# Gathers of 127 rows instead of 128 in a graph layer's aggregation

## The chip, the core and the metric

The kernel runs on one core of a Trainium2 chip. The metric is the device time of one execution in microseconds, the median of several runs.

## What is computed

One graph layer over 50,000 nodes of 128 features and 1,650,000 edges that are sorted by destination. Every edge carries its source's row through one of two linear maps, chosen by the edge's type; the messages are summed by destination, the node's own row is mapped and added, and relu, a residual and a layer norm follow.

```
Xs = X[src]
m_data = Xs @ W_data.T + b_data
m_ctrl = Xs @ W_control.T + b_control
msg = jnp.where((edge_types == 0)[:, None], m_data, m_ctrl)
agg = jax.ops.segment_sum(msg, dst, num_segments=X.shape[0])
out = agg + (X @ W_self.T + b_self)
x = _layernorm(x + relu(out), axis=-1)
```

All of it is float32; in the graph, 800,000 random pairs are taken both ways and each node has a loop.

## The kernel before

The maps are linear, so the kernel sums source rows first and maps the sums. Edges are cut into chunks of 128 (12,891 of them, the last with 80 edges), 14 chunks to a step, 921 steps, 20 steps to a group. Since edges are sorted, a step's destinations fall into a window of W = 64 nodes that starts at `base`.

For each chunk, `products` (L158 to L171) issues one indirect DMA on GpSimd's queue (L166): edge e's source row of x, 512 bytes, lands in partition e of a tile y. TensorE multiplies y by a one-hot matrix of 128 columns, 64 nodes by two edge types (L169), and accumulates over the step's 14 chunks in PSUM. A last product with ones (L170) turns the counts of edges into a multiple of the bias. A float32 product shows as two MATMUL instructions.

The one-hot comes from `onehot` (L146 to L155), on VectorE: one comparison for all 14 chunks (L151) and one reduction for the counts (L154), three steps ahead of its use (AHEAD). `columns` (L123 to L138) makes, once per group, the column number of each edge, and the smallest and largest of them for a check at the end. `carry` (L185 to L189) adds to a step's sums what the step before had beyond its own window; `layer` (L199 to L206) maps the sums, `moments` and `store` do the norm and write 64 rows.

The order is written out by hand at the end of `straight` (L228 to L250): in the loop over steps come the carry and transpose of the step before, the load of x's rows for four steps later (`window`, SP's queue), in the middle of a group the three loads of edges for the next one (`load_edges`, L82 to L86, SP's queue), then this step's products, the layer of the step before, the moments of the one before that, the one-hot of three steps ahead, and the store. GpSimd has hardly anything but the gathers. The tile pool of y has 5 * S = 70 buffers, and edge tiles have two.

If the check at the end finds a destination outside of its window, `general` (from L277 on) computes all again in another way; on this graph it isn't run.

The edge arrays are laid out on the host as [128, chunks]: partition p of column c is edge 128 c + p.

## Time and profile before

| | before |
|---|---|
| median of 2 runs | 18587.68 us (18585.29 to 18590.06) |
| profiled execution, its own time | 16137.76 us |
| its span, first to last instruction | 16136.0 us |
| PE busy | 12545.0 us (78%) |
| POOL busy | 12182.1 us (75%), 12,891 gathers of 945 ns |
| VectorE busy | 6216.3 us (39%) |
| granted clock of TensorE | 0.52 |
| moved by DMA | 935.47 MB, 58 GB/s |

The profile shows one execution. PE is TensorE's products and PEld its weight loads, DVE is VectorE, ACT ScalarE, POOL GpSimd, SP the engine that issues plain DMAs. Of an indirect DMA on POOL, the busy time is what the engine spends on the instruction, and the transfer comes after it. A group's line gives the line number, engine, operation, tiles (out<-in) and count, then busy time, mean ns of one, and the idle time of the engine just before with what ended it. The runs take longer than the profiled execution, so both are given.

### The profile page before, as it was taken

How to read it: one execution, taken by the hardware profiler on the slowest of the kernel's cores; microseconds unless marked ns; L12 is line 12 of the kernel's file. 1: busy time of each engine (PE TensorE's matmuls, PEld its weight loads, DVE VectorE, ACT ScalarE, POOL GpSimd, SP SyncE). 2: the span in 40 equal slices, each digit the busy share in tenths (PEclk: the TensorE clock that was granted, in tenths of full speed). 3: DMA queues.
4: the chain of work that ended last, by engine and by line, in shares of the span. 5: the costliest groups of instructions: out<-in, count | busy, mean ns of one | idle time of the engine just before them, and what ended most of it. 6: DMA issues, size and time to landing. Idle time of an engine off the chain costs nothing.

```text
span 16136.0 us, 131172 instructions
## 1 busy us (share of the span) xinstructions
PE 12545.0 (78%) x39604; PEld 8196.0 (51%) x39605; DVE 6216.3 (39%) x7631; ACT 470.5 (3%) x1848; POOL 12182.1 (75%) x12899
## 2 busy tenths in 40 slices
PE   7777777777777777777777777777777777777777
PEld 4555555555555555555555555555555555555554
DVE  4333333333333333333333333333333333333333
ACT  0000000000000000000000000000000000000000
POOL 7777777777777777777777777777777777777777
PEclk5555555555555555555555555555555555555555
DMA  2222222222222222222222222222222222222222
GB/s 60 58 58 59 58 58 58 58 58 59 58 58 58 58 58 58 59 58 58 58 58 58 59 58 58 58 58 58 58 59 58 58 58 58 58 58 59 58 58 55
DMA packets 581475, 935.47 MB, mean 58 GB/s; under 512 B 238051, under 2 KB 374374, under 8 KB 580758
## 3 DMA queue, kind: packets, MB, share of 16 engines
q0 software_dynamic: 412512, 845.63, 20.1%
q1 hardware_dynamic: 167808, 81.17, 1.9%
q8 instruction: 318, 5.21, 0.1%
q14 instruction: 399, 3.27, 0.1%
q10 hardware_dynamic: 438, 0.20, 0.0%
HBM read 895.86 MB, written 30.18 MB: 57 GB/s over the span
## 4 chain that ended last, share of the span: by engine, by line
DMA 43%; PE 39%; issue 14%; POOL 4%; POOLq 0%; DVE 0%; ACT 0%; ACTq 0%
DMA y<-in_x,idx_g 43%; PE acc L169 17%; PE po L205 6%; PE po L206 6%; POOL y L166 4%; PE po L202 3%; PE po L203 3%; PE acc L170 2%; PE px L194 1%; POOLq L166 0%; DMA idx_g<-in_src_t 0%; DVE o L225 0%; ACT sd L217 0%; DVE h L211 0%; POOL num L107 0%
## 5 line engine op out<-in xcount | busy, mean ns | idle before, releaser
L166 POOL DMA_INDIRECT y<-in_x,idx_g x12891 | 12181.1, 945 | 3928.8 <-issue 1768.6
L169 PE MATMUL acc<-oh,y 128*128 128x128 f32 x25782 | 8534.1, 469 | 3568.3 <-DMA y<-in_x,idx_g 3543.7
L169 PEld LDWEIGHTS acc<-oh,y 128*128 128x128 f32 x25782 | 6054.6, 312 | 5885.3 <-DMA y<-in_x,idx_g 5709.2
L189 DVE TENSOR_TENSOR sums<-acc,sums 128x256 f32<-128x256 f32 x921 | 391.0, 425 | 6746.0 <-PE acc L170 6746.0
L154 DVE TENSOR_REDUCE cnt<-oh 128x128 f32<-128x1792 f32 x921 | 2922.5, 3173 | 31.7
L151 DVE TENSOR_TENSOR oh<-col_g,num_ps 128x1792 f32<-128x1792 f32 x921 | 1824.3, 1981 | 0.0
L211 DVE SCALAR_TENSOR_TENSOR h<-po,xw 64x128 f32<-64x128 f32 x921 | 260.7, 283 | 3013.4 <-PE po L206 3013.4
L205 PE MATMUL po<-wmsgT,sums 128*64 128x128 f32 x3684 | 1269.8, 448 | 3.3 <-DVE sums L189 3.3
L206 PE MATMUL po<-bias,sums 1*64 1x128 f32 x3684 | 1260.6, 444 | 0.0
L205 PEld LDWEIGHTS po<-wmsgT,sums 128*64 128x64 f32 x3684 | 531.7, 204 | 610.9 <-issue 606.9
L206 PEld LDWEIGHTS po<-bias,sums 1*64 1x64 f32 x3684 | 523.7, 202 | 608.8 <-issue 608.8
L196 ACT COPY xT<-px 128x64 f32<-128x64 f32 x921 | 195.9, 213 | 15325.7 <-PE px L194 15325.7
L202 PE MATMUL po<-wselfT,xT 128*64 128x128 f32 x1842 | 635.6, 449 | 0.2 <-ACT xT L196 0.2
L203 PE MATMUL po<-bias,ones 1*64 1x128 f32 x1842 | 630.3, 444 | 0.0
L170 PE MATMUL acc<-cnt,ones 128*128 128x128 f32 x1842 | 584.1, 421 | 0.0
L170 PEld LDWEIGHTS acc<-cnt,ones 128*128 128x128 f32 x1842 | 503.5, 333 | 0.0
L203 PEld LDWEIGHTS po<-bias,ones 1*64 1x64 f32 x1842 | 261.9, 202 | 304.4 <-issue 304.4
L202 PEld LDWEIGHTS po<-wselfT,xT 128*64 128x64 f32 x1842 | 266.6, 205 | 206.9 <-issue 206.5
L194 PE MATMUL px<-ident,xw 64*128 64x64 f32 x921 | 336.1, 365 | 0.0
L225 DVE TENSOR_SCALAR o<-h,mv,rstd 64x128 f32<-64x128 f32 x921 | 317.6, 345 | 33.3
L194 PEld LDWEIGHTS px<-ident,xw 64*128 64x128 f32 x921 | 163.9, 178 | 303.6 <-issue 303.4
L217 ACT ACTIVATE sd<-mv,eps 64x1 f32<-64x1 f32 x921 | 271.3, 295 | 322.1 <-DVE mv L215 318.2
(56 smaller groups left out, 667.8 us busy)
## 6 DMA issues: line engine op xcount, KB each, us to landing
y<-in_x,idx_g POOLq DMA_INDIRECT x12891, 2.5
xw<-in_x SPq DMA_DIRECT2D x921, 32.0 KB
out<-o SPq DMA_DIRECT2D x921, 32.0 KB
idx_g<-in_src_t SPq DMA_DIRECT2D x47, 140.0 KB
d_g<-in_dst_t SPq DMA_DIRECT2D x47, 140.0 KB
t_g<-in_edge_type_t SPq DMA_DIRECT2D x47, 140.0 KB
first_i<-in_dst_first SPq DMA_DIRECT2D x1, 460.5 KB
w_sb<-in_L_gnn_W_data ACTq DMA_DIRECT2D x1, 64.0 KB
```

The source lines that it names most:

```text
L151: nc.vector.tensor_tensor(oh[:, :n, :], col_g[g][:, i, :n, None].to_broadcast([P, n, 2 * W]), num_ps[:, None, :].to_broadcast([P, n, 2 * W ...
L154: nc.vector.tensor_reduce(cnt, oh[:, :n, :].rearrange("p s w -> p w s"), AX.X, ALU.add)
L166: nc.gpsimd.indirect_dma_start(out=y[:r], out_offset=None, in_=x, in_offset=bass.IndirectOffsetOnAxis(ap=idx_g[g][:r, i, k:k + 1], axis=0))
L169: nc.tensor.matmul(flat[:, :2 * W], y[:r], oh[:r, k, :], start=k == 0, stop=k == n - 1)
L170: nc.tensor.matmul(flat[:, 2 * W:], ones, cnt, start=True, stop=True)
L189: nc.vector.tensor_tensor(sums[s % RING][:, :, :W], accs.pop(s), sums[(s - 1) % RING][:, :, bass.ds(d, W)], op=ALU.add)
L194: nc.tensor.transpose(px, xws[s], c["ident"][:W, :W])
L202: nc.tensor.matmul(po, xTs.pop(s), c["wselfT"], start=True, stop=False)
L203: nc.tensor.matmul(po, ones[0:1, :W], bias[:, 2, :], start=False, stop=False)
L205: nc.tensor.matmul(po, a[:, t, :W], c["wmsgT"][:, t * D:(t + 1) * D], start=False, stop=False)
L206: nc.tensor.matmul(po, a[0:1, 2 + t, :W], bias[:, t, :], start=False, stop=t == 1)
L225: nc.vector.tensor_scalar(o, hs.pop(s), mv[:, 0:1], rstd, op0=ALU.subtract, op1=ALU.mult)
```

## The change

A new constant R = 127 takes the place of 128 as the number of edges in a chunk. There are 12,993 chunks, the last with 16 edges, and 929 steps. All tiles of edges and the one-hot have 127 partitions, as has y; products contract over 127 rows. The tile of the check's numbers, which is reduced over all 128 partitions at the end, is set to zero first. The host lays the edges out as [127, chunks]. The other path (`general`) keeps its chunks of 128.

```diff
+R = 127
+NCHUNK = -(-E // R)
+LAST = E - (NCHUNK - 1) * R
...
     stats = keep.tile([P, 2, GROUPS], F32, name="stats")
+    nc.vector.memset(stats, 0.0)
...
-            t = eds.tile([P, GS, S], I32, name=name)
+            t = eds.tile([R, GS, S], I32, name=name)
             nc.sync.dma_start(t.rearrange("p a b -> p (a b)"), a[:, g * GS * S:(g + 1) * GS * S])
...
-        oh = ohp.tile([P, S, 2 * W], F32, name="oh")
-        nc.vector.tensor_tensor(oh[:, :n, :], col_g[g][:, i, :n, None].to_broadcast([P, n, 2 * W]),
-                                num_ps[:, None, :].to_broadcast([P, n, 2 * W]), op=ALU.is_equal)
-        cnt = ohp.tile([P, 2 * W], F32, name="cnt")
+        oh = ohp.tile([R, S, 2 * W], F32, name="oh")
+        nc.vector.tensor_tensor(oh[:, :n, :], col_g[g][:, i, :n, None].to_broadcast([R, n, 2 * W]),
+                                num_ps[:R, None, :].to_broadcast([R, n, 2 * W]), op=ALU.is_equal)
+        cnt = ohp.tile([R, 2 * W], F32, name="cnt")
...
-            r = LAST if s * S + k == NCHUNK - 1 else P
-            y = gat.tile([P, D], F32, name="y")
+            r = LAST if s * S + k == NCHUNK - 1 else R
+            y = gat.tile([R, D], F32, name="y")
             nc.gpsimd.indirect_dma_start(
                 out=y[:r], out_offset=None, in_=x,
                 in_offset=bass.IndirectOffsetOnAxis(ap=idx_g[g][:r, i, k:k + 1], axis=0))
             nc.tensor.matmul(flat[:, :2 * W], y[:r], oh[:r, k, :], start=k == 0, stop=k == n - 1)
-        nc.tensor.matmul(flat[:, 2 * W:], ones, cnt, start=True, stop=True)
+        nc.tensor.matmul(flat[:, 2 * W:], ones[:R], cnt, start=True, stop=True)
...
-        arrays[k + "_t"] = np.ascontiguousarray(a[:TCH * CH].reshape(TCH, CH).T)
-    arrays["dst_first"] = np.ascontiguousarray(arrays["dst"][:STEPS * S * CH:S * CH])
+        arrays[k + "_t"] = np.ascontiguousarray(a[:TCH * R].reshape(TCH, R).T)
+    arrays["dst_first"] = np.ascontiguousarray(arrays["dst"][:STEPS * S * R:S * R])
```

The tiles of `columns` change in the same way.

More of the change, by code (lines that the diff above doesn't have):

```diff
@@ L27 @@
 CH = 128
-NCHUNK = -(-E // CH)
-LAST = E - (NCHUNK - 1) * CH
 DST_PAD = 65536
+R = 127
+NCHUNK = -(-E // R)
+LAST = E - (NCHUNK - 1) * R
 W = 64
@@ L41 @@
 U = 35
-CPP = -(-(NCHUNK + U) // P)
+CPP = -(-(-(-E // CH) + U) // P)
 NCH = CPP * P
@@ L125, in columns @@
         d, t = d_g.pop(g), t_g.pop(g)
-        rel = eds.tile([P, GS, S], F32, name="rel")
-        nc.vector.tensor_tensor(rel, d, base[:, g * GS:(g + 1) * GS, None].to_broadcast([P, GS, S]),
+        rel = eds.tile([R, GS, S], F32, name="rel")
+        nc.vector.tensor_tensor(rel, d, base[:R, g * GS:(g + 1) * GS, None].to_broadcast([R, GS, S]),
                                 op=ALU.subtract)
-        col = eds.tile([P, GS, S], F32, name="col_g")
+        col = eds.tile([R, GS, S], F32, name="col_g")
         nc.vector.tensor_scalar(col, t, 0.0, float(W), op0=ALU.not_equal, op1=ALU.mult)
@@ L133, in columns @@
         if g == GROUPS - 1:
-            chk = eds.tile([P, GS, S], F32, name="chk")
+            chk = eds.tile([R, GS, S], F32, name="chk")
             nc.vector.scalar_tensor_tensor(chk, d, float(DST_PAD), rel, op0=ALU.is_lt, op1=ALU.mult)
-        nc.vector.tensor_reduce(stats[:, 0, g:g + 1], chk.rearrange("p a b -> p (a b)"), AX.X, ALU.min)
-        nc.vector.tensor_reduce(stats[:, 1, g:g + 1], chk.rearrange("p a b -> p (a b)"), AX.X, ALU.max)
+        nc.vector.tensor_reduce(stats[:R, 0, g:g + 1], chk.rearrange("p a b -> p (a b)"), AX.X, ALU.min)
+        nc.vector.tensor_reduce(stats[:R, 1, g:g + 1], chk.rearrange("p a b -> p (a b)"), AX.X, ALU.max)
         col_g[g] = col
@@ L559 @@
     for k, pad in (("src", 0), ("dst", DST_PAD), ("edge_type_2", 0)):
-        a = np.pad(np.asarray(inputs[k], dtype=np.int32), (0, max(EPAD, TCH * CH) - E), constant_values=pad)
+        a = np.pad(np.asarray(inputs[k], dtype=np.int32), (0, max(EPAD, TCH * R) - E), constant_values=pad)
         arrays[k] = np.ascontiguousarray(a[:EPAD])
-        arrays[k + "_t"] = np.ascontiguousarray(a[:TCH * CH].reshape(TCH, CH).T)
-    arrays["dst_first"] = np.ascontiguousarray(arrays["dst"][:STEPS * S * CH:S * CH])
+        arrays[k + "_t"] = np.ascontiguousarray(a[:TCH * R].reshape(TCH, R).T)
+    arrays["dst_first"] = np.ascontiguousarray(arrays["dst"][:STEPS * S * R:S * R])
     nc = bacc.Bacc("TRN2", target_bir_lowering=False, num_devices=1)
```

## The prediction

> **What bounds the kernel now.** I read the page's busy shares and costliest groups first, then what POOL waits for, the transfers, and two stretches of the timeline. Page, parts 1 and 3 to 5:

> ```profile
> PE 12545.0 (78%) x39604; PEld 8196.0 (51%) x39605; DVE 6216.3 (39%) x7631; ACT 470.5 (3%) x1848; POOL 12182.1 (75%) x12899
> ...
> q0 software_dynamic: 412512, 845.63, 20.1%
> q1 hardware_dynamic: 167808, 81.17, 1.9%
> ...
> DMA 43%; PE 39%; issue 14%; POOL 4%; POOLq 0%; DVE 0%; ACT 0%; ACTq 0%
> ...
> L166 POOL DMA_INDIRECT y<-in_x,idx_g x12891 | 12181.1, 945 | 3928.8 <-issue 1768.6
> L169 PE MATMUL acc<-oh,y 128*128 128x128 f32 x25782 | 8534.1, 469 | 3568.3 <-DMA y<-in_x,idx_g 3543.7
> ```

> PE has the larger busy share, and the chain names transfers (43%) and PE (39%). The groups say otherwise: PE's gap before L169 is a wait for y, and POOL's busy time plus its gap before L166, 12181.1 + 3928.8 = 16109.9 us, is the span (16136.0) but for 26 us. The waits of POOL:

> ```profile
> POOL y L166 <- issue: 1768.6, 5806, 0.3
> POOL y L166 <- PE acc L169: 1226.1, 4025, 0.3
> POOL y L166 <- DMA y<-in_x,idx_g: 694.2, 2279, 0.3
> ```

> Whatever releaser is named, no wait is over 0.3 us: 3928.8 / 12891 = 0.305 us stands before every gather, so it is a fixed part of issuing one. The period is 16110 / 12891 = 1.250 us, from first to last. The end of the timeline (start, length, engine, line), where the last gather has 80 rows and not 128:

> ```profile
> 16108.20 0.94 POOL L166 DMA_INDIRECT y<-in_x,idx_g  x1 [0.30 <-issue]
> ...
> 16109.45 0.94 POOL L166 DMA_INDIRECT y<-in_x,idx_g  x1 [0.30 <-issue]
> ...
> 16110.70 0.91 POOL L166 DMA_INDIRECT y<-in_x,idx_g  x1 [0.30 <-issue]
> ...
> 16113.19 0.80 PE L169 MATMUL acc<-oh,y 80*128 80x128 f32 x2 [0.41 <-DMA y<-in_x,idx_g]
> ```

> The view of tile y gives 907 ns as the shortest gather and 945 as the median. So 48 rows fewer save 38 ns: 0.8 ns a row, or 12.7 ns for each 16 rows. Rows taken linearly cost 8 x 12.7 = 101 ns, and 844 ns don't depend on them. That is the number on which the forecast turns: the change takes one row in 128 and perhaps fifteen engines in sixteen.

> How far PE is behind, in the timeline:

> ```profile
> 8000.70 0.64 PE L170 MATMUL acc<-cnt,ones 128*128 128x128 f32 x2
> ...
> 8005.26 3.31 PE L169 MATMUL acc<-oh,y 128*128 128x128 f32 x12
> ...
> 8022.88 3.05 PE L169 MATMUL acc<-oh,y 128*128 128x128 f32 x12
> ```

> What PE does once per step takes from 8000.70 to 8005.26, 4.56 us. Twelve unstarved products take 3.05 us, (3.05 - 0.42) / 11 = 0.239 each; 28 are 6.7 us. PE needs 11.3 us of the step's 14 x 1.25 = 17.5: a floor of 0.80 us per gather. DVE needs 6216.3 / 921 = 6.7 us per step.

> [...] 412512 / 12891 = 32 packets a gather and 845.63 MB / 12891 = 65.6 KB, that is sixteen 4 KB packets and sixteen of 4 bytes. For 127 rows nothing here shows it. [...]

> **The change, part by part.**

> *More gathers.* 1,650,000 / 127 gives 12993 for 12891: 102 more, 0.79%. At 1.250 us each that is +127 us of the profiled span. The last one has 16 rows. Steps are 929 for 921; the eight add 8 x 11.3 us to PE and 8 x 6.7 to DVE, behind POOL's period, so nothing. If POOL fell below 0.80 us they'd count 90 us on PE.

> *One row less per gather.* 1 x 0.8 ns x 12993 = -10 us if cost goes by rows. If it goes by rounds of 16, 127 rows are still eight and nothing is saved.

> *One engine for sixteen.* Not in the trace. Bounds: below, the 844 + 305 ns contain per-engine work of which 15/16 goes, 1.08 us; but PE then stops it at 0.80 us per gather. Above, the 12.7 ns are a round that serves sixteen engines at once, and one engine takes 127 rounds: (127 - 8) x 12.7 = +1511 ns. I take zero, from between the bounds: [...]

> *The transfer itself.* It has 20.1% of 16 x 16136 / 12891 = 4.03 us of engine time a gather. On one engine this is serial: landing goes from 2.5 to about 2.5 + 4.03 x 15/16 = 6.3 us. 70 buffers of y hold 70 x 1.25 = 87 us, [...]. Hidden; [...].

> *Edge loads (L85).* 127 partitions on SP's queue: [...]. q1's packets take 1.9% of 16 x 16136 / 167808 = 29 ns at 484 bytes on average; 127 of 1120 bytes are an estimated 4 to 9 us, three loads 11 to 26. They are issued ten steps (175 us) early, three SP issues as before, and SP's queue behind them holds rows of x four steps ahead. Hidden, but for the first: gather one waits for idx_g, now 2.3 us, so +4 to +9 once.

> *DVE and PE on 127 partitions.* Same free sizes, so the same time; the memset of stats is one instruction. No new wait stands in any loop.

> Sum, profiled: +127 + 6 - 10 to 0, so about 16136 + 128 = 16264. The median of the runs is 18587.68, 1.152 times the profiled execution's 16137.76, or 1.442 us a gather. [...] I carry the ratio: 18587.68 x 12993 / 12891 = 18735 us, +0.8%.

> **The cases.**

> *U, nothing but more gathers* (24%): 18735, own range 18600 to 18950. [...]

> *F2, a pass over sixteen engines falls away* (23%). If the 0.305 us before each gather is such a pass, 15/16 of it is 0.286: 0.964 us, 12993 x 0.964 = 12.53 ms, 14430 us in runs; with part of it, up to 18300. For it: the gap is constant and the same for all releasers. [...] It beats 2% from 0.035 us saved.

> *F1, [...]* (13%): POOL drops to PE's floor, 929 x 11.3 us = 10.5 ms, 12100 us in runs. For it: 844 of 945 ns don't follow rows. [...]

> *S1, rounds per engine* (20%), the other side: at L166 each gather makes 127 rounds of 12.7 ns, so 1.250 + 1.511 = 2.761 us; 12993 of them 35.9 ms, 41300 us in runs. It decides from 0.13 ns per extra round (0.015 us for 2%). [...] Against it: one measured point, the 80-row gather.

> *S2, the same with cheaper rounds* (17%): half of S1's, 2.0 us, 26.0 ms, 30000 us; from 19000 to 36000.

> *S3, [...]* (3%): 4.03 us, 52.4 ms, 60300 us.

> **How the numbers follow.** Faster 0.36 (F1, F2), within 2% 0.24 (U), slower 0.40 (S1 to S3). About 2% is what a measurement of this kernel can tell from no change. U is the likeliest single case, hence 18735, though both signs weigh more than it; its own range is above. Range 13000 to 42000: below lies most of F1 (0.10), above S3 and S1's upper part (0.08).

> **What would show it.** L166's mean near 945 and 0.30 before it in a count of 12993: U. A shorter gap: F2; a shorter L166: F1, with PE's waits for y gone. An L166 of 1.5 to 2.5 us with PE waiting for y at every product: S. q0's packets tell k: 32 a gather with sixteen of about 4 KB either way, so landing decides: 2.5 us if spread, some 6 us on one engine. A profiled execution whose ratio to the runs isn't 1.15 would break my conversion. I am wrong wherever a 127-row gather takes POOL over 2% more or less than a 128-row one.

## The result, and the profile after

| | before | after |
|---|---|---|
| median of the runs | 18587.68 us | 37101.58 us (37101.0 to 37102.17, 2 runs) |
| profiled execution, its own time | 16137.76 us | 37101.0 us |
| span | 16136.0 us | 37099.2 us |
| gathers, POOL's time of one | 12,891 of 945 ns | 12,993 of 2548 ns |
| gather, issue to landing (median) | 2.5 us | 7.7 us |
| granted clock of TensorE | 0.52 | 0.50 |

The change makes the kernel slower: the ratio of the runs is 1.996 (95% interval 1.9874 to 2.0046). The runs of the kernel before differ between the comparisons, which were made on different chips: 16.14 ms in that of e1 to e4 below, 18.6 ms in the others. The kernel after took 37.1 ms in both of its comparisons, which were of the 18.6 ms kind. The profile of before is of a 16.14 ms execution, and whether that was on the chip of its two runs isn't known. So the two traces differ by a factor of 2.30.

The page of the kernel after, parts 1 and 3 to 5:

```profile
PE 14174.4 (38%) x39928; PEld 8641.5 (23%) x39929; DVE 6789.8 (18%) x7696; ACT 475.1 (1%) x1864; POOL 33103.5 (89%) x13001
...
q0 software_dynamic: 3533856, 944.63, 16.1%
...
DMA 61%; POOL 24%; PE 10%; issue 5%; POOLq 0%; DVE 0%; ACT 0%; ACTq 0%
...
L168 POOL DMA_INDIRECT y<-in_x,idx_g x12993 | 33102.6, 2548 | 3967.9 <-issue 2159.9
L171 PE MATMUL acc<-oh,y 127*128 127x128 f32 x25986 | 10128.4, 498 | 22906.0 <-DMA y<-in_x,idx_g 22856.3
```

POOL is the bound, as in the profile before: 33102.6 + 3967.9 = 37070.5 us is the span but for 29 us, 2.853 us a gather for 1.250. The gap ahead of a gather is the same 3967.9 / 12993 = 0.305 us; all that grew is the instruction, by 1.603 us. 12993 x 1.603 = 20.83 ms, and 102 more gathers at 1.25 us are 0.13 ms: together 20.96, the difference of the spans (37099.2 - 16136.0 = 20963 us) to the last 10 us. PE's wait for y goes from 3543.7 to 22856.3 us and is only the other face of this. The chain puts 61% on the transfer of y, and again it is no limit: POOL's waits stay at 0.3 us.

```profile
POOL y L168 <- issue: 2159.9, 7087, 0.3
POOL y L168 <- PE acc L171: 1777.4, 5831, 0.3
POOL y L168 <- DMA y<-in_x,idx_g: 18.9, 62, 0.3
```

The queue's line has the mechanism in it. 3533856 / 12993 = 272 packets a gather, for 32 before, and 944.63 MB / 12993 = 72.70 KB, though 127 rows are only 65.02. The packet records of the trace have, per gather: sixteen packets for the rows (15 of 4096 bytes, one of 3584), sixteen of 4 bytes, and 240 of 32 or 28 bytes. The last are 15 x 127 x 4 = 7620 bytes, fifteen times 15 packets of 32 and one of 28, beside the 65024 of the rows: 65024 + 7620 + 64 = 72708. In the trace of before, a gather's sixteen row packets start within 0.31 us of each other (median) and are done 0.53 us after the first start. Here those of the last gather of 127 rows follow one another from 37071.93 to 37075.57 us, each starting within 10 ns of the end of the one before, and a gather's row packets take 3.62 us together on average. So one engine carries all rows, and the small packets fit fifteen others with as many entries as it has, 127 of 4 bytes each (an entry stands here for one row's piece of work for one engine). The last gather, in the timeline, has 16 rows in sixteen packets of 512 bytes, so it is spread over sixteen engines:

```profile
37068.36 2.55 POOL L168 DMA_INDIRECT y<-in_x,idx_g  x1 [0.31 <-issue]
37071.21 0.86 POOL L168 DMA_INDIRECT y<-in_x,idx_g  x1 [0.30 <-issue]
```

If an instruction is made of rounds of sixteen entries, one for each engine, the last gather has one round and takes 863 ns, and the others have 127 and take 2548: 1685 / 126 = 13.4 ns a round.

### The profile page after: what moved, and what is told of

It is laid out like the page before. It is cut to its first block, busy times and chain, and to the rows that moved or that the text cites. A ratio compares the mean times of both kernels' runs of the same rounds, so it can differ in the third digit from the quotient of the medians.

```text
span 37099.2 us, 132247 instructions
## 1 busy us (share of the span) xinstructions
PE 14174.4 (38%) x39928; PEld 8641.5 (23%) x39929; DVE 6789.8 (18%) x7696; ACT 475.1 (1%) x1864; POOL 33103.5 (89%) x13001
## 3 DMA queue, kind: packets, MB, share of 16 engines
q0 software_dynamic: 3533856, 944.63, 16.1%
## 4 chain that ended last, share of the span: by engine, by line
DMA 61%; POOL 24%; PE 10%; issue 5%; POOLq 0%; DVE 0%; ACT 0%; ACTq 0%
DMA y<-in_x,idx_g 61%; POOL y L168 24%; PE acc L171 7%; PE po L207 1%; PE po L208 1%; PE po L204 0%; PE po L205 0%; PE acc L172 0%; PE px L196 0%; POOLq L168 0%; DMA idx_g<-in_src_t 0%; DVE o L227 0%; ACT sd L219 0%; DVE st L215 0%; POOL num L109 0%
## 5 line engine op out<-in xcount | busy, mean ns | idle before, releaser
L168 POOL DMA_INDIRECT y<-in_x,idx_g x12993 | 33102.6, 2548 | 3967.9 <-issue 2159.9
L171 PE MATMUL acc<-oh,y 127*128 127x128 f32 x25986 | 10128.4, 498 | 22906.0 <-DMA y<-in_x,idx_g 22856.3
L171 PEld LDWEIGHTS acc<-oh,y 127*128 127x128 f32 x25986 | 6476.7, 311 | 26393.5 <-DMA y<-in_x,idx_g 26229.0
L156 DVE TENSOR_REDUCE cnt<-oh 127x128 f32<-127x1792 f32 x929 | 2932.7, 3157 | 32.0
L153 DVE TENSOR_TENSOR oh<-col_g,num_ps 127x1792 f32<-127x1792 f32 x929 | 1838.5, 1979 | 0.0
L227 DVE TENSOR_SCALAR o<-h,mv,rstd 64x128 f32<-64x128 f32 x929 | 845.7, 910 | 33.4
L213 DVE SCALAR_TENSOR_TENSOR h<-po,xw 64x128 f32<-64x128 f32 x929 | 262.4, 282 | 3039.3 <-PE po L208 3039.3
L172 PE MATMUL acc<-cnt,ones 127*128 127x128 f32 x1858 | 589.3, 421 | 0.0
L172 PEld LDWEIGHTS acc<-cnt,ones 127*128 127x128 f32 x1858 | 507.7, 333 | 0.2 <-issue 0.2
L215 DVE BATCH_NORM_STATS2 st<-h 64x6 f32<-64x128 f32 x929 | 265.3, 286 | 32.1
```

Of the source, the lines that this page charges most:

```text
L153: nc.vector.tensor_tensor(oh[:, :n, :], col_g[g][:, i, :n, None].to_broadcast([R, n, 2 * W]), num_ps[:R, None, :].to_broadcast([R, n, 2 * ...
L156: nc.vector.tensor_reduce(cnt, oh[:, :n, :].rearrange("p s w -> p w s"), AX.X, ALU.add)
L168: nc.gpsimd.indirect_dma_start(out=y[:r], out_offset=None, in_=x, in_offset=bass.IndirectOffsetOnAxis(ap=idx_g[g][:r, i, k:k + 1], axis=0))
L171: nc.tensor.matmul(flat[:, :2 * W], y[:r], oh[:r, k, :], start=k == 0, stop=k == n - 1)
L172: nc.tensor.matmul(flat[:, 2 * W:], ones[:R], cnt, start=True, stop=True)
L227: nc.vector.tensor_scalar(o, hs.pop(s), mv[:, 0:1], rstd, op0=ALU.subtract, op1=ALU.mult)
```

## The experiments

The theory (T in the expectations), an estimate from 2548 ns and 863: POOL's instruction is made of such rounds, and a gather of r rows over k engines takes r / k rounds of some 13 ns on top of some 850 ns. The rivals: something else in the change (O), a single engine alone on a slow path (P), POOL held by the speed at which one engine takes rows (L).

**e1_g128: the change without the odd row count.** Chunks of 127 edges, but gathers of 128 rows: the tile of row numbers has a 128th partition that repeats the last, and the products leave its row out.

```diff
-            y = gat.tile([R, D], F32, name="y")
+            y = gat.tile([P, D], F32, name="y")
...
-                out=y[:r], out_offset=None, in_=x,
-                in_offset=bass.IndirectOffsetOnAxis(ap=idx_g[g][:r, i, k:k + 1], axis=0))
+                out=y, out_offset=None, in_=x,
+                in_offset=bass.IndirectOffsetOnAxis(ap=idx_g[g][:, i, k:k + 1], axis=0))
```

> Chunks of 127 edges as in the changed kernel, but each gather has 128 rows (the last index is taken twice, its row isn't used). Theory T, rounds: a gather of r rows on k engines holds POOL for 850 ns + 13.4 ns x r/k (from the changed kernel: 2548 ns at 127 rounds, 863 at one), so it falls back to about 945 ns, 12993 gathers of 1.25 us are 16.24 ms profiled, 0.8% over the kernel before. Theory O, something else in the change (127 partitions in products, one-hots and edge loads): stays near 37 ms.

16267.34 us against 16135.87 of the kernel before in the same comparison: 1.0081 (1.0064 to 1.0098). Its gathers take 945 ns and POOL's gap is the old one:

```profile
L168 POOL DMA_INDIRECT y<-in_x,idx_g x12993 | 12274.8, 945 | 3961.1 <-issue 1681.7
```

The 102 more gathers are 0.79%. So the change without the row count of the gather (and with the row numbers loaded on 128 partitions) costs what the number of gathers says, and O falls.

**e6_b127: the odd row count without the change.** The kernel before with 127 of each chunk's 128 rows gathered; the last edge of a chunk is left out of the sums.

```diff
-            r = LAST if s * S + k == NCHUNK - 1 else P
+            r = LAST if s * S + k == NCHUNK - 1 else P - 1
```

> The kernel before with nothing changed but the number of rows of a gather, 127 of the 128 (the last edge of every chunk is left out of the sums). Theory T, rounds: 2548 ns a gather, 12891 of them 2.853 us apart, 36.8 ms. Theory O, the layout of the change: 945 ns and 16.1 ms.

36804.45 us, 2548 ns a gather:

```profile
L166 POOL DMA_INDIRECT y<-in_x,idx_g x12891 | 32844.4, 2548 | 3931.9 <-issue 3286.9
```

One row less, alone, makes the gather 2.7 times as long, and the kernel 1.97 times as long as the 18656.59 us of its own comparison (2.28 times the 16135.87 of e1's).

**e2_r126 and e3_r120: other row counts.** Only R is changed, to 126 and 120.

> R = 126: two engines divide it, 63 rows each. Theory T: 850 + 63 x 13.4 = 1694 ns of POOL per gather, 2.00 us apart, 13096 gathers, 26.2 ms. Theory P, only a gather on a single engine is taken on a slow path: about 945 ns, 16.4 ms.

> R = 120: eight engines, 15 rows each. Theory T: 850 + 15 x 13.4 = 1051 ns, 1.356 us apart, 13750 gathers, 18.6 ms profiled. Theory P: 945 ns, 17.2 ms.

17062.75 and 17733.96 us: neither the 26.2 nor the 18.6 ms foretold. The pages' lines, e2_r126 first:

```profile
q0 software_dynamic: 628592, 846.58, 19.8%
...
L168 POOL DMA_INDIRECT y<-in_x,idx_g x13096 | 13043.1, 996 | 3989.8 <-issue 1925.8
```

```profile
q0 software_dynamic: 440000, 846.12, 19.0%
...
L168 POOL DMA_INDIRECT y<-in_x,idx_g x13750 | 13505.7, 982 | 4195.4 <-issue 1954.7
```

I had taken k as the largest power of two; the packets say otherwise. With 120 rows a gather has 440000 / 13750 = 32 packets: fifteen of 4096 bytes, one of 32 for an idle engine, sixteen of 4. With 126 there are 48: fourteen engines with 9 rows (4096 + 512 bytes), two idle ones with 32 + 4. So k is 15 and 14, in both the largest divisor of the row count up to 16, and the rounds are 8 and 9. At T's 850 + 13.4 x rounds this makes 957 and 971 ns, and both take 25 ns more, which T has no term for. As these runs turned out they don't tell T from P.

**e7_r125 and e8_r122: 25 and 61 rounds.** Only R is changed again: 125 is 5 x 25, 122 is 2 x 61.

> R = 125: five engines of 25 rows. From 982 ns at 8 rounds on 15 engines, 996 at 9 rounds on 14 and 2548 at 127 rounds on one: 877 + 13.2 x rounds. Theory T: 877 + 25 x 13.2 = 1207 ns, 1.512 us apart, 13200 gathers, 19.96 ms. Theory P, a single engine alone is slow: about 990 ns, 1.295 us apart, 17.1 ms.

> R = 122: two engines of 61 rows. Theory T: 877 + 61 x 13.2 = 1682 ns, 1.987 us apart, 13525 gathers, 26.9 ms. Theory P, a single engine alone is slow: about 990 ns, 17.5 ms.

20029.11 and 26707.22 us, with 1211 and 1667 ns a gather (1207 and 1682 foretold), e7_r125 first:

```profile
L168 POOL DMA_INDIRECT y<-in_x,idx_g x13200 | 15978.7, 1211 | 4027.9 <-issue 2467.2
```

```profile
L168 POOL DMA_INDIRECT y<-in_x,idx_g x13525 | 22551.7, 1667 | 4126.7 <-issue 2588.2
```

P falls: gathers of 125 and 122 rows take longer too, by what 25 and 61 rounds foretell. The last gathers of e2_r126 and e8_r122, of 30 and 72 rows, add two points. All row counts together; the engines of 16, 80, 120, 126, 127 and 128 rows are read from packets, those of 30, 72, 112, 122 and 125 are an estimate, the largest divisor up to 16 as in the others:

| rows | engines | rounds | POOL, ns a gather | from |
|---|---|---|---|---|
| 16 | 16 | 1 | 863 | last gather of after |
| 30 | 15 | 2 | 906 | last gather of e2_r126 |
| 80 | 16 | 5 | 907 | last gather of before |
| 72 | 12 | 6 | 945 | last gather of e8_r122 |
| 112 | 16 | 7 | 936 | e10_r112 |
| 128 | 16 | 8 | 945 | before |
| 120 | 15 | 8 | 982 | e3_r120 |
| 126 | 14 | 9 | 996 | e2_r126 |
| 125 | 5 | 25 | 1211 | e7_r125 |
| 122 | 2 | 61 | 1667 | e8_r122 |
| 127 | 1 | 127 | 2548 | after |

Two things stay open. Eight rounds take 945 ns on sixteen engines and 982 on fifteen, but at 61 rounds 850 + 13.4 x 61 = 1667 is met without an extra: what fewer than sixteen engines add isn't one fixed number, and nothing here shows what it is. And since the bytes of an idle engine are 4 for each row of a busy one (508 for 127 rows, 36 for 9, 32 for 8), there seem to be sixteen entries to a round whatever k is. Sixteen at once in 13.4 ns, or one after the other in 0.84 ns each, would look the same in these runs.

**e4_half127: half the bytes.** The kernel after with gathers of 256 bytes a row; the sums are of other data than the reference's.

```diff
-                out=y[:r], out_offset=None, in_=x,
+                out=y[:r], out_offset=None, in_=x.rearrange("n (h d) -> (n h) d", h=2),
...
-            nc.tensor.matmul(flat[:, :2 * W], y[:r], oh[:r, k, :], start=k == 0, stop=k == n - 1)
+            for h in range(2):
+                nc.tensor.matmul(flat[h * W:(h + 1) * W, :2 * W], y[:r], oh[:r, k, :], start=k == 0, stop=k == n - 1)
```

> The changed kernel with gathers of 256 bytes per row in place of 512 (x read as 100,000 half rows, each product done twice on 64 features; what is summed is another thing than the reference). Theory T: [...] 2548 ns a gather and 37.1 ms as before. Theory L, POOL is held by how fast one engine takes its rows: half the bytes, so about half of the extra 1.6 us goes, 1.7 us a gather, 26 ms.

37108.55 us, 2548 ns to the nanosecond, while landing falls from 7.7 to 6.0 us:

```profile
L168 POOL DMA_INDIRECT y<-in_x,idx_g x12993 | 33108.9, 2548 | 3969.3 <-issue 3709.1
```

The packets of one gather's rows take 2.10 us of their engine's time in place of 3.62. L falls, by bytes and by rows: POOL isn't held by the engine that takes them.

**e5_after_again and e9_before_again: the two kernels once more**, since the runs of before had taken 18588 us and its profiled execution 16138.

> The changed kernel unaltered, beside the kernel before on one chip. If the median of the kernel before in the first comparison (18588 us) was a matter of that comparison, the ratio is 2.30 (37101 to 16136); if it belongs to the kernel, some executions of it are near 18588 here too and the ratio is between 2.0 and 2.3.

37110.34 us against 18656.59 in that comparison: 1.9891 (1.9858 to 1.9924). So the first ratio is met again; against the 16135.87 of e1's comparison it is 2.30. All seven runs of before lay within 5 us of each other here, and all seven within 3 us there, so within a comparison single executions don't differ. No chip that is known was used for two comparisons, so whether the chip or something else about the comparison decides isn't shown.

> The kernel before unaltered, profiled once more, since its runs took 18588, 16136 and 18657 us in three comparisons while kernels with slower gathers took what rounds foretell in all of them. Theory C, POOL's own work: where it takes 18.6 ms, L166 or the gap before it is longer, 1.44 us in all. Theory D, a second limit near 1.44 us a gather that lies elsewhere (transfers or products): L166 stays at 945 ns and POOL waits for buffers, with a named engine and waits over 0.3 us. Where it takes 16.1 ms, neither is seen.

18593.15 us, so this profile has what the first one lacked:

```profile
L166 POOL DMA_INDIRECT y<-in_x,idx_g x12891 | 12171.0, 944 | 6371.5 <-issue 3141.7
L169 PE MATMUL acc<-oh,y 128*128 128x128 f32 x25782 | 6345.5, 399 | 3795.9 <-issue 3498.9
```

A gather takes 944 ns as ever, but the idle time before it has gone from 3928.8 to 6371.5 us, and PE now has waits for nothing that the profile shows (issue) where it had waited for y. POOL's waits in this run:

```profile
POOL y L166 <- issue: 3141.7, 9975, 3.3
POOL y L166 <- PE acc L169: 1631.9, 1426, 5.1
POOL y L166 <- remote: 1191.1, 834, 4.8
```

Three quarters of them stay at 3141.7 / 9975 = 0.31 us. The time that is new lies in fewer and longer waits, put down to PE and to a releaser that the trace doesn't know as an engine of this core (remote). So POOL's own work isn't longer, and C falls; this is D of the expectation, a second limit outside of it.

**e10_r112, e11_halfpe, e12_bufs8: what the second limit goes by.** R = 112; every second product of L169 left out, so that half of the edges aren't summed; 8 buffers for y in place of 70.

```diff
-            nc.tensor.matmul(flat[:, :2 * W], y[:r], oh[:r, k, :], start=k == 0, stop=k == n - 1)
+            if k % 2 == 0:
+                nc.tensor.matmul(flat[:, :2 * W], y[:r], oh[:r, k, :], start=k == 0, stop=k >= n - 2)
```

```diff
-    gat = ctx.enter_context(tc.tile_pool(name="gat", bufs=5 * S))
+    gat = ctx.enter_context(tc.tile_pool(name="gat", bufs=8))
```

> R = 112: sixteen engines of 7 rows, one round less than before. Theory T: 850 + 7 x 13 = about 935 ns, 1.24 us apart, 14733 gathers, 18.27 ms, that is 1.13 times a kernel before that takes 16.14 ms: a shorter gather isn't worth its count. Where the kernel before takes 18.6 ms, theory C gives about 21.1 ms (the same 1.43 us a gather), theory D with a limit that goes by bytes about 18.6 ms.

> The kernel before with every second product on gathered rows left out (half of the edges are not summed; all gathers are made). Theory E, where the kernel before takes 18.6 ms PE sets the pace, standing still for 1 to 3 us ahead of single products: with 14 product instructions less per step POOL's pace is the bound again, 16.1 ms. Theory N, the limit lies in the gathers or transfers: 18.6 ms stays. Beside a kernel before of 16.1 ms, both give 16.1 ms.

> The kernel before with 8 buffers for y in place of 70. Theory E with a trigger, the standstills come after PE has run through a backlog of landed rows at the full clock: 8 tiles allow no such backlog, so 16.1 to 16.6 ms where the kernel before takes 18.6 ms. If the standstills need no backlog, PE stays the bound and POOL waits more often for buffers: 18.6 ms or longer. Beside a kernel before of 16.1 ms: 16.1 to 16.4 ms.

21239.4, 18490.93 and 18631.23 us, all beside a kernel before of 18.59 ms. By steps of 14 gathers the four spans are alike: 18591.3 / 921 = 20.19 us for before, 21239.8 / 1053 = 20.17, 18488.6 / 921 = 20.07, 18635.0 / 921 = 20.23. Fewer rows a gather, half the products, a ninth of the buffers: none moves it. Its number for e10 is the one that I had foretold for C, but POOL's instruction is 936 ns there and its waits for nothing shown are 0.31 us on average (3393.6 / 10803), so C is wrong all the same. Both forms of E, that PE sets the pace and that a backlog of landed rows sets the standstills off, fall with e11 and e12. Nor does the limit need PE's waits for nothing shown, or stretches at the full clock: ahead of L169 these waits are 3498.9 us in e9_before_again and 148.6 in e12_bufs8, PE had the full clock for 2956 and 618 us (642 in the 16.14 ms profile), and both are as slow. N has the number of e11, but nothing shows its mechanism: in e10 an eighth less data per gather, in as many gathers a step, left the step as long.

What stands late can be seen in the timeline of e12_bufs8:

```profile
8016.08 0.69 PE L206 MATMUL po<-bias,sums 1*64 1x128 f32 x2
...
8022.22 0.28 DVE L211 SCALAR_TENSOR_TENSOR h<-po,xw 64x128 f32<-64x128 f32 x1 [8.69 <-PE acc L169]
...
8022.98 0.21 ACT L196 COPY xT<-px 128x64 f32<-128x64 f32 x1 [19.05 <-PE acc L169]
...
8023.20 0.95 POOL L166 DMA_INDIRECT y<-in_x,idx_g  x1 [2.96 <-PE acc L169]
```

L211 needs what L206 ended at 8016.77 by the records, and starts 5.45 us later; then ACT and POOL, which wait for other work of PE, come free within a microsecond. In the first profile of before, at the same time of the run, L206 ends at 8005.04 and L211 starts at 8005.07:

```profile
8004.35 0.69 PE L206 MATMUL po<-bias,sums 1*64 1x128 f32 x2
...
8005.07 0.28 DVE L211 SCALAR_TENSOR_TENSOR h<-po,xw 64x128 f32<-64x128 f32 x1 [3.28 <-PE po L206]
```

In e11_halfpe L212, the same instruction, waits up to 33.9 us, more than a step, for a releaser that the trace calls remote; the longest wait of L211 in the first profile was 3.3 us. So by the records word of PE's work arrives late in these executions, in the stretch of e12_bufs8 once a step. Whether PE itself stands still (its ends are modelled in the records) or only its signals are held, and why there, is open; so is why the sum comes to 20.2 us a step. No version here that sums all edges beats the kernel before.

## Why the prediction was right or wrong

**The bound** was read rightly: POOL's period, not PE's larger busy share nor the chain's transfers. It is the bound after, too. (Where the kernel before takes 18.6 ms it isn't that kernel's bound; see the last point below.)

**More gathers:** right. 0.79% foretold, a ratio of 1.0081 measured once the gathers were left at 128 rows (e1_g128).

**One engine for sixteen** is the step that failed. Between its two bounds I took zero, which no trace had shown. All rows went to one engine. The sixteen packets of 4 bytes that a gather has in the trace of before stay (206256 for 12891 gathers, 207888 for 12993), but that speaks only against a gain. The term that I put at nothing was 1.603 us a gather. The upper bound was the answer: 12.7 ns a round by the 80-row gather, 13.4 by the 127-row one; 1.511 us more foretold in S1, 1.603 measured; a period of 2.761 us foretold, 2.853 measured. The headline of 18735 us was thus half of what came, and what came true was S1, to which I gave 20%. The range reached to 42000 for S1's sake alone, so that it holds the result says nothing for the account behind the headline. I had the evidence in hand: 48 rows in 38 ns, 12.7 for each 16, fit rounds of sixteen better than the reading of 844 ns as work by engines.

**F1 and F2**, a gain by engines that fall away: wrong. The gap of 0.305 us, which F2 took for a pass over sixteen engines, is the same with one, and the instruction, which F1 had shrink with the engines, grows from 945 to 2548 ns.

**The transfer, hidden:** right; no wait of POOL over 0.3 us names it, and it isn't the same engine for every gather: the sixteen row packets of a gather take 3.62 us, more than one engine could give every 2.853 us, and packets of two gathers overlap (those of the last but one of 127 rows end at 37072.74 us, those of the last begin at 37071.93). So S3, with one engine's 4.03 us as the period of all gathers, falls. Landing was put at 6.3 us and is 7.7. POOL's longer instruction seems to lie in it, by an estimate: 2.5 us of before, 1.6 more of the instruction and 15 more packets of 0.23 make about 7.6.

**Edge loads:** hidden but for the first, as foretold; POOL's first wait for idx_g goes from 2.3 to 8.0 us, within the 4 to 9 more. That estimate takes a load's packets one after the other, and 127 of 1120 bytes at the 49 ns that the records show (median) are 6.2 us. What I missed is that SP's third load of a group now takes 7.0 us to issue for 0.4; nothing waits for it.

**VectorE and PE on 127 partitions:** the same time, as foretold. The comparison takes 1979 ns for 1981 and the reduction 3157 for 3173; a starved pair of product instructions takes 0.79 to 0.80 us, as in e12_bufs8 on 128.

**The ratio of runs to profile**, 1.152, carried over as if all work took longer: wrong. What stands behind it is a limit of its own at 20.2 us a step, which a POOL period of 2.853 us (40 us a step) covers entirely, and S1's 35.9 ms should not have been raised to 41.3. The records show no engine's own work longer by anything near 15%: in e9_before_again POOL's 944 ns, VectorE's L154 (3185 ns for 3173) and ScalarE's L217 (295 for 295) are as before, and PE's products are shorter (399 ns for 469). And had F1 or F2 come true, this limit would by e10 to e12 have left nothing of the gain in executions of the 18.6 ms kind.

## What to carry to other kernels

In the row counts run here, the time of a gather's instruction on GpSimd goes by rows per engine, from 863 ns at one to 2548 at 127, and wherever the packets were read the number of engines is the largest divisor of the row count up to 16. So try a multiple of 16 first: 112 rows took 936 ns and 128 took 945, but the prime 127 took 2548. Of these two multiples the larger is better, since by the estimate above some 850 ns of each gather don't depend on its rows. When one odd-sized instance in the trace gives a slope, ask per what unit that slope is (row, round, engine), for a change of shape will pull the readings apart. A ratio between runs and profile is a finding to be explained before it is used as a factor.

## What the runs showed of the hardware

A gather under way holds VectorE up where it scales the rows of the output (L227; L225 in the kernel before, L228 in e4_half127). The instruction, 64 x 128 floats from and to SBUF, took 345 ns on average before; these are its lines in the lists of groups of the kernel before, of e7_r125, of the kernel after and of e4_half127:

```profile
L225 DVE TENSOR_SCALAR o<-h,mv,rstd 64x128 f32<-64x128 f32 x921 | 317.6, 345 | 33.3
```

```profile
L227 DVE TENSOR_SCALAR o<-h,mv,rstd 64x128 f32<-64x128 f32 x943 | 489.3, 519 | 34.0
```

```profile
L227 DVE TENSOR_SCALAR o<-h,mv,rstd 64x128 f32<-64x128 f32 x929 | 845.7, 910 | 33.4
```

```profile
L228 DVE TENSOR_SCALAR o<-h,mv,rstd 64x128 f32<-64x128 f32 x929 | 441.4, 475 | 33.4
```

It takes 519 ns with gathers of 1211 and 910 with gathers of 2548, while L213 beside it, which reads PSUM too, stays at 282 to 283. But the mean doesn't go by the gather's length alone: with the same 2548 ns it is 475 in e4_half127 and 680 in e6_b127, and 629 with the 1667 ns of e8_r122. The records of the single instructions show why. Every one that takes over 400 ns (892 in the kernel after, 825 in e6_b127, 894 in e7_r125, 353 in e8_r122) starts 0.44 us or more into a gather and ends 19 to 45 ns after that gather's end; the 585 of e8_r122 that start earlier in a gather take 335 to 341 ns. So it waits for the gather's instruction to end, and the mean is set by where in the gather it happens to start.

Why it has to, no view shows. VectorE is far from the bound (18%), so it costs nothing here.
